# A state-space convolution with a gated low-rank layer behind it: tables formed as they lie from group 3 on, products of zeros at the start, and two short chains on GpSimd

## The chip, the cores and the metric

The kernel runs on one core of one Trainium2 chip. A core has a matrix engine (TensorE, PE in the profile, with its weight loads as PEld), a vector engine (VectorE, DVE), a scalar engine for activations and copies (ScalarE, ACT), a general engine (GpSimd, POOL) and a queue engine that issues transfers (SyncE, SP). They run side by side and wait for each other by semaphores. The metric is the device time of one execution in microseconds; lower is better. Before the change it is 955.25 us, the median of three runs from 955.22 to 955.43.

## The reference

```python
x = x + ffn(cond(x, length, log_dt, C, log_A_real, A_imag, D), A, B, Wr)

# cond: a state-space convolution, H = 64 heads, N = 64 states a head, 64 rows, L = 1024
A = -exp(log_A_real) + 1j * A_imag
dtA = A * exp(log_dt)[:, None]
Cs = Cc * (exp(dtA) - 1.0) / A
K = 2.0 * einsum('hn,hnl->hl', Cs, exp(dtA[:, :, None] * arange(L))).real
y = (causal convolution of x * mask with K) + x * mask * D
y = y * mask

# ffn: 64 experts of rank 16, 16 of them chosen for each token
scores = y @ Wr.T
gates = softmax(top_k(scores, 16)), 0 elsewhere
out = einsum('nkr,kdr->nd', einsum('nd,krd->nkr', y, A) * gates, B) * 2.0
```

All of it is computed in float32.

## The kernel before

**Tiling.** The 64 heads are worked on in eight groups of eight (`NG = 8`, `HG = 8`), and a group's heads in four pairs (`GP = 4`): the 64 states of two heads fill 128 partitions. The 1024 places of a row are cut into eight blocks of 128 (`P = 128`, `NBLK = 8`).

**The convolution of a group, `conv(g)` (L660).** Inside a block it is a product with a Toeplitz matrix `toep` (L695). Across blocks it goes over states. `into_states` (L631) multiplies the input of a pair by the table `bt`, which holds, for each of the 128 places of a block, the factor with which that place enters each state: two matmuls for each of the real and the imaginary part (L642, tile `pu`), and a copy by ScalarE into `s` (L647). `recur` (L674) carries the states from block to block on VectorE, by `turn`. `across` (L700) multiplies the states by the table `w` into the same PSUM banks `pc` as the Toeplitz product (L704), and VectorE multiplies the sum by the mask into `y` (L712). Group 0 does all this by itself; from group 1 on `begin(g)` (L650) forms the states of the next group at the end of the `conv` before.

**The tables, `tables(g)` (L241).** A generator, which is run step by step (to its next `yield`) from within `conv` of the group before. Its first eight steps make, for 129 places `lv` along the free axis and the states on the partitions, the magnitude `mag` (exponentials on ScalarE, L253), the angle `f` in turns (L255 and on, VectorE), its sines (L268 to L271, ScalarE) and from these the real and imaginary part of `w`. Then `w` is multiplied by each state's `alpha` and `nbeta`: two ScalarE products (L353) and two VectorE operations (helper line L400) a pair, into tiles `b` with the states on the partitions. Since the matmul into the states needs the places on the partitions, `turned_table` (L333) transposes them on TensorE, eight 128x128 transposes a group (L338, tile `pb`), and ScalarE copies them into `bt` (L340). After that come `turn`, the sum of `bt` over the states (`kernels_by_vector`, L304), which gives the convolution's kernel, and its way through DRAM into `toep` (L315 to L320).

The tiles `mag`, `f`, `k` and `sn` of `tables` exist once each (`tabp`, one buffer): a new tile of the same name waits until the old one has been read for the last time.

**The steps.** From group 1 on `conv(g)` runs `step(4)` after the recurrence of pairs 0 and 1 (L746), `step(6)` after that of pairs 2 and 3 (L755), and `step(1)` (L761) ahead of `begin(g + 1)`.

**The layer behind.** `first(g)` (L842) multiplies `y` by the first low-rank factor with seven products of half-size blocks in place of eight (`seven`, L577, the matmul of L587, tile `h`), `gates` (L766) makes the scores and the gates, GpSimd multiplies by the gates `gx` (L857), and `second` (L936) does the same with the second factor (L1095) for all groups at the end. The products of `first` are generators too and are laid between the steps of the next group's `conv`.

**The start.** VectorE and ScalarE follow an order written by hand here (`manual_schedule`, L438 and L440): `exp_parts` (L415) for the step sizes and decay rates, then, taken in turns by `together` (L403), the first steps of `tables(0)`, `real_part` (L472) and `angle` (L479), then `products` (L517), which ends with `alpha`, `nbeta` and `nalpha`. In the meantime TensorE adds quarters of the first factor by products with the identity (`factors_by_identity`, L187, L195), as the quarters land; ScalarE copies these sums (L200, L204).

**Order.** Where no order is written by hand, a scheduler sets each engine's order before the run, out of the program's order and estimated times. At run time each engine and each queue takes its instructions strictly in that order; SP's queue carries the loads of `x` (L147) and the transfers of `krows` and `toep`.

Of the kernel before, what the change touches and what calls it, by code (L numbers as in the profile page):

```python
# [37 lines left out]
F32 = mybir.dt.float32  # L38
I32 = mybir.dt.int32
AF = mybir.ActivationFunctionType  # L40
ALU = mybir.AluOpType
# [3 lines left out]
P = 128  # L45
NB = 64
NH = 64
L = 1024
# [14 lines left out]
NP = NH // 2  # L63
GP = HG // 2
NW = P + 1
NCH = NBLK - 1
# [3 lines left out]
MAGIC = 12582912.0  # L70
INV_HI = 5.0 / 32.0
INV_LO = INV2PI - INV_HI
HALF_IN = 0.49999997
# [19 lines left out]
def body(ctx: ExitStack, tc, x, xo, lens, par, dvec, dgrp, at, bm, wt, cst, out):  # L93
    nc = tc.nc
    V = nc.vector
    G = nc.gpsimd
# [90 lines left out]
    def factors_by_identity(a21, a22, a11, a12, out):  # L187


        s1, s2, s4 = (factor(wp, "wa", t) for t in ("s1", "s2", "s4"))  # L190
        out.extend((a11, a12, s4, a22, s1, s2, a21))
        banks = [ps_f.tile([P, L // 2], F32, tag="pf", name=f"sum_{k}") for k in range(KH)]

        def add(bank, a, first=False, last=False):
            nc.tensor.matmul(bank, lhsT=ident, rhs=a, start=first, stop=last, skip_group_check=True)  # L195

        for k in range(KH):
            add(banks[k], a21[:, k, :], first=True)
            add(banks[k], a22[:, k, :])
            nc.scalar.copy(s1[:, k, :], banks[k])  # L200
            yield
        for k in range(KH):
            add(banks[k], a11[:, k, :], last=True)
            nc.scalar.copy(s2[:, k, :], banks[k])  # L204
            yield
# [30 lines left out]

    tabs = {}
    turned = {}
    scales = {}

    def tables(g):  # L241
# [80 lines left out]
        def rows(ks, i, n):  # L322
# [5 lines left out]
            nc.sync.dma_start(toep[:, 2 * i : 2 * n, :],  # L328
                              bass.AP(row.tensor, row.offset, [[1, P], [KROW, 2 * (n - i)], [1, P]]))

        bbs, halves = [], []

        def turned_table(i, n):  # L333

# [4 lines left out]
                                        bbs[(i + m) // 2][:, (i + m) % 2, c, :], ident)  # L339
            nc.scalar.copy(bt[:, i : i + n, :], pb)  # L340

        for i in range(GP):
            j = j0 + i
            re, im = w[:, 0, i, :P], w[:, 1, i, :P]
            if i % 2 == 0:
                bb = tabp.tile([P, 2, 2, P], F32, tag=("sn", "k")[i // 2], name=f"b_{g}_{i}")
                bbs.append(bb)
            b = bb[:, i % 2]
            for c, by in enumerate((alpha, nbeta)):
                if g == 0:  # L350
                    ts(b[:, c, :], re, by[:, j : j + 1], ALU.mult)
                else:
                    nc.scalar.activation(b[:, c, :], re, AF.Copy, scale=by[:, j : j + 1])  # L353
            stt(b[:, 0, :], im, nbeta[:, j : j + 1], ALU.mult, b[:, 0, :], ALU.add)
            stt(b[:, 1, :], im, nalpha[:, j : j + 1], ALU.mult, b[:, 1, :], ALU.add)
            if g:
                if i % 2:
                    yield
                continue
            turned_table(i, 1)  # L360
            if i % 2:
                halves.append(kernels(bbs[i // 2 :], i - 1))
            if i == 3:
                rows(*halves[0])
            yield
        if g:
            turn, toep = others()
            for i in (0, 2):
                turned_table(i, 2)
            turned[g] = bt  # L370
            yield
# [12 lines left out]
    def new(name, w=NP, dtype=F32, keep=False):  # L384
        pool = const if keep else prep
        return pool.tile([P, w], dtype, tag=f"p_{name}", name=f"p_{name}")

    def tt(o, a, b, o_):
        V.tensor_tensor(out=o, in0=a, in1=b, op=o_)  # L389
        return o  # L390

    def ts(o, a, s1, o1, s2=None, o2=None):
        if o2 is None:
            V.tensor_scalar(out=o, in0=a, scalar1=s1, scalar2=None, op0=o1)
        else:
            V.tensor_scalar(out=o, in0=a, scalar1=s1, scalar2=s2, op0=o1, op1=o2)
        return o

    def stt(o, a, s, o1, b, o2):
        V.scalar_tensor_tensor(out=o, in0=a, scalar=s, in1=b, op0=o1, op1=o2)  # L400
        return o
# [10 lines left out]
        for _ in range(n):  # L412
            yield next(it, None)

    def exp_parts(xin, name, w, out):  # L415

        xc = ts(new(name + "x", w), xin, -87.0, ALU.max, 88.0, ALU.min)
        k = ts(new(name + "k", w), xc, LOG2E, ALU.mult)
        yield
        ts(k, k, MAGIC, ALU.add, MAGIC, ALU.subtract)  # L420
        yield
        stt(xc, k, -LN2_HI, ALU.mult, xc, ALU.add)
        yield
        stt(xc, k, -LN2_LO, ALU.mult, xc, ALU.add)
        s = new(name + "s", w, I32)
        ts(s, k, 127.0, ALU.add, 8388608.0, ALU.mult)
        yield
        q = ts(new(name + "q", w), xc, 1.0 / math.factorial(8), ALU.mult)
        for i in range(7, 0, -1):
            yield  # L430
            stt(q, q, 1.0 / math.factorial(i), ALU.add, xc, ALU.mult)
        out += [s.bitcast(F32), q]
# [5 lines left out]
    first_order.enter_context(tc.manual_schedule(engines={V.engine}))  # L438
    first_copies = ExitStack()
    first_copies.enter_context(tc.manual_schedule(engines={nc.scalar.engine}))  # L440
    log_both = par_sb[:, 0:2, :].rearrange("p a h -> p (a h)")
    a_im, c_re, c_im = (par_sb[:, i, :] for i in (2, 3, 4))
    parts = []
# [28 lines left out]
    def real_part():  # L472
# [3 lines left out]
        yield  # L476
        stt(em1, parts[0], -1.0, ALU.add, em1, ALU.add)

    def angle():  # L479
        ts(r, turns, MAGIC, ALU.add, MAGIC, ALU.subtract)  # L480
        yield
        tt(r, tu_hi, r, ALU.subtract)
        yield
        tt(r, r, tu_lo, ALU.add)
        yield
        ts(r, r, HALF_IN, ALU.min, -HALF_IN, ALU.max)
        nc.scalar.activation(sin, r, AF.Sin, scale=2.0 * math.pi)
        nc.scalar.activation(s2, r, AF.Sin, scale=math.pi)
        yield
        tt(den, a_re, a_re, ALU.mult)  # L490
        yield
        tt(t1, a_im, a_im, ALU.mult)
        yield
        tt(den, den, t1, ALU.add)
        yield
        V.reciprocal(rden, den)
        yield
        tt(s2, s2, s2, ALU.mult)
        yield
        ts(s2, s2, 2.0, ALU.mult)  # L500

    wa, wb = [], []
    marks = {}
# [13 lines left out]
    def products():  # L517
        ts(e_re, s2, -1.0, ALU.mult, 1.0, ALU.add)
        stt(e_im, em1, 1.0, ALU.add, sin, ALU.mult)
        yield  # L520
        tt(e_re, e_re, em1, ALU.mult)
        tt(t1, e_im, a_im, ALU.mult)
        tt(n_im, e_im, a_re, ALU.mult)
        yield
        tt(e_re, e_re, s2, ALU.subtract)
        yield
        tt(n_re, e_re, a_re, ALU.mult)
        tt(t2, e_re, a_im, ALU.mult)
        yield
        tt(n_re, n_re, t1, ALU.add)  # L530
        tt(n_im, n_im, t2, ALU.subtract)
        yield
        tt(n_re, n_re, rden, ALU.mult)
        tt(n_im, n_im, rden, ALU.mult)
        yield
        tt(alpha, c_re, n_re, ALU.mult)
        tt(t1, c_im, n_im, ALU.mult)
        tt(beta, c_re, n_im, ALU.mult)
        tt(t2, c_im, n_re, ALU.mult)
        yield  # L540
        tt(alpha, alpha, t1, ALU.subtract)
        tt(beta, beta, t2, ALU.add)
        yield
        ts(alpha, alpha, 2.0, ALU.mult)
        ts(nbeta, beta, -2.0, ALU.mult)
        ts(nalpha, alpha, -1.0, ALU.mult)

    together(products(), some(steps0, 2))
# [111 lines left out]
    def conv(g, steps, out):  # L660
# [39 lines left out]
        def across(i, s, pcs, pinned=False):  # L700
            for c in range(2):
                for hh in range(2):
                    o = hh * NS
                    m = nc.tensor.matmul(  # L704
                        pcs[hh][:, NB:], lhsT=w[o : o + NS, c, i, 1:],
                        rhs=s[o : o + NS, c].rearrange("p k b -> p (k b)"),
                        start=False, stop=(c == 1),
                    )
                    if pinned:
                        tc.keep_in_program_order(m)  # L710
            for hh in range(2):
                marks["y"] = V.tensor_tensor(  # L712
                    out=y[:, :, i // 2, 2 * (i % 2) + hh, :],
                    in0=pcs[hh].rearrange("p (k b) -> p k b", b=NB), in1=mask, op=ALU.mult)

        def step(n):
            for _ in range(n):
                next(steps, None)
# [14 lines left out]
        if g == 0:  # L733
            into_states(0, 2, bt, states, more)
            into_states(0, 3, bt, states, more)
            first_two = inside(0), inside(1)
            across(*first_two[0], True)
            across(*first_two[1])
            recur(2, 3)
            last_two = inside(2), inside(3)  # L740
            yield
            across(*last_two[0], True)
            across(*last_two[1])
            return
        yield
        step(4)  # L746
        yield 2

        first_two = inside(0), inside(1)
# [481 lines left out]
    def flat(t, i, w):  # L1231
        return t[:, i : i + w * HT].rearrange("p (k t) -> p k t", t=HT)
# [13 lines left out]
    n = 0  # L1246
# [84 lines left out]
```

## Time and profile before

One execution was taken by the profiler. Times are in us.

| | |
|---|---|
| median of three runs | 955.25 |
| the profiled execution: its time, and its span from first to last instruction | 955.27, 953.5 |
| TensorE busy (matmuls) | 942.5, 99% |
| VectorE busy | 714.3, 75% |
| GpSimd busy | 332.5, 35% |
| ScalarE busy | 150.8, 16% |
| transfers | 143.97 MB, mean 151 GB/s |
| transposes into `pb` (L338) | 64 instructions, 9.6 busy |
| copies into `bt` (L340), 128x512 | 14, 7.5 busy |
| ScalarE products into `b` (L353) | 56, 21.7 busy |
| VectorE operations into `b` (L400) | 64, 22.0 busy |
| recurrence (L400 into `s` and `s_more`) | 576, 172.7 busy |

Busy time is the union of an engine's instructions. A single instruction's time includes the pipeline's ends, so the distance between two starts is often shorter than the duration. A wait is named as "engine line waited for: us in total, times, longest". Helper lines stand for many operations: L389 is any VectorE operation with two tensors, L396 and L394 one with a tensor and numbers, L400 one with a tensor, a number and a tensor. The numbers of the tiles' copies are left out, so `was` is any tile of the first factor whose name begins so.

### The profile page before, as it was taken

To read this page: it belongs to the slowest core of one execution; us is meant where nothing else is said; L and a number is where in the kernel's file an instruction comes from. 1 tells how busy PE (TensorE), PEld (TensorE's weight loads), DVE (VectorE), ACT (ScalarE), POOL (GpSimd) and SP (SyncE) were. 2 spreads that over 40 slices of the span, in tenths; PEclk is the share of its full clock that TensorE was granted. 3 is DMA by queue.
4 is the path that set the end of the run, shared out by engine and by line. 5 is a ranking of instruction groups with operands and counts; after the bars stand their busy time and mean duration, and the time that the engine had idled before them with its cause. 6 is when DMAs were issued, how large, how long until landed. Compare 5 with 4: busy or idle time off the path is not lost. (4 is left out here: it accounts for less than half of the span.)

```text
span 953.5 us, 11891 instructions
## 1 busy us (share of the span) xinstructions
PE 942.5 (99%) x4259; PEld 725.4 (76%) x4259; DVE 714.3 (75%) x1697; ACT 150.8 (16%) x302; POOL 332.5 (35%) x285
## 2 busy tenths in 40 slices
PE   7999999999999999999999999999999999999998
PEld 2476767587587587587587688888888888888887
DVE  8899798695794795695594399869856865786674
ACT  5343233401401401311200000000000000000000
POOL 0212204042042041042132132257745554764565
PEclk9999999999999999999999999999999999999999
DMA  8815326235243244334323274653683475268332
GB/s 287 228 41 166 120 78 172 83 108 164 89 142 129 89 116 138 106 105 133 121 69 126 95 268 149 244 221 102 221 296 89 166 265 188 84 214 299 110 119 102
DMA packets 68985, 143.97 MB, mean 151 GB/s; under 512 B 9472, under 2 KB 20288, under 8 KB 68928
## 3 DMA queue, kind: packets, MB, share of 16 engines
q1 hardware_dynamic: 49420, 94.40, 29.5%
q0 software_dynamic: 16864, 47.22, 15.4%
q10 hardware_dynamic: 2644, 1.61, 0.6%
q8 instruction: 33, 0.54, 0.2%
q14 instruction: 24, 0.20, 0.1%
HBM read 94.89 MB, written 47.25 MB: 149 GB/s over the span
## 5 line engine op out<-in xcount | busy, mean ns | idle before, releaser
L400 DVE SCALAR_TENSOR_TENSOR s<-s,turn 128x64 f32<-128x64 f32 (+1 forms) x432 | 118.9, 320 | 3.5 <-ACT s L647 2.4
L857 POOL TENSOR_TENSOR hg<-h_p,gx 128x512 f32<-128x512 f32 x16 | 29.3, 1829 | 258.0 <-DVE h_p L400 251.9
L587 PE MATMUL h<-y,waa 128*128 128x256 f32 x512 | 118.7, 381 | 0.0
L587 PE MATMUL h<-y,was 128*128 128x256 f32 x512 | 116.5, 380 | 0.0
L587 PE MATMUL h<-ty,was 128*128 128x256 f32 x512 | 116.0, 379 | 0.0
L587 PEld LDWEIGHTS h<-y,waa 128*128 128x128 f32 x512 | 95.6, 190 | 20.0 <-issue 6.9
L587 PEld LDWEIGHTS h<-y,was 128*128 128x128 f32 x512 | 96.7, 190 | 15.0 <-issue 1.5
L587 PEld LDWEIGHTS h<-ty,was 128*128 128x128 f32 x512 | 97.1, 190 | 13.9 <-issue 0.8
L712 DVE TENSOR_TENSOR y<-pc,mask 128x512 f32<-128x512 f32 x64 | 41.1, 684 | 52.3 <-PE pc L704 52.3
L857 POOL TENSOR_TENSOR hg<-h_u,gx 128x512 f32<-128x512 f32 x32 | 46.7, 1460 | 78.8 <-DVE h_u L389 73.7
L1109 ACT COPY p<-s 128x512 f32<-128x512 f32 x28 | 16.4, 586 | 312.4 <-PE s L1095 312.4
L954 POOL TENSOR_TENSOR o<-o,acc_a 128x512 f32<-128x512 f32 x32 | 47.6, 1506 | 41.4 <-ACT acc_a L972 21.6
L389 DVE TENSOR_TENSOR h_u<-h,h_u 128x512 f32<-128x512 f32 x48 | 32.8, 683 | 35.3 <-PE h L587 35.3
L587 PE MATMUL h<-ty,waa 128*128 128x256 f32 x256 | 58.4, 381 | 0.0
L695 PE MATMUL pc<-x,toep 128*128 128x512 f32 x128 | 57.7, 594 | 0.0
L587 PEld LDWEIGHTS h<-ty,waa 128*128 128x128 f32 x256 | 48.2, 190 | 9.6 <-DVE y L712 3.3
L954 POOL TENSOR_TENSOR o<-o,b_room 128x512 f32<-128x512 f32 x32 | 49.1, 1556 | 9.8 <-DVE b_room L389 9.8
L830 POOL DMA_DIRECT2D gx<-gt_dram x56 | 33.9, 620 | 51.5 <-DMA gt_dram<-gt 51.5
L389 DVE TENSOR_TENSOR o<-o,s 128x512 f32<-128x512 f32 x50 | 34.1, 681 | 23.1 <-PE s L1095 17.9
L642 PE MATMUL pu<-x,bt 128*64 128x448 f32 x256 | 51.1, 545 | 0.0
L389 DVE TENSOR_TENSOR hg<-hg 128x512 f32<-128x512 f32 x64 | 42.5, 684 | 10.5 <-POOL hg L857 9.9
L954 POOL TENSOR_TENSOR o<-o,u 128x512 f32<-128x512 f32 x36 | 45.3, 1281 | 10.0 <-DVE u L389 9.7
(238 smaller groups left out, 1612.5 us busy)
## 6 DMA issues: line engine op xcount, KB each, us to landing
x<-in_x SPq DMA_DIRECT2D x32, 512.0 KB
hg_dram<-hg POOLq DMA_DIRECT2D x16, 1024.0 KB, 5.6
o<-in_xo SPq DMA_DIRECT2D x64, 256.0 KB
out<-o SPq DMA_DIRECT2D x63, 256.0 KB
gx<-gt_dram POOLq DMA_DIRECT2D x56, 256.0 KB, 4.8
qy<-hg_dram SPq DMA_DIRECT2D x28, 512.0 KB
r<-hg_dram SPq DMA_DIRECT2D x26, 512.0 KB
hg_dram<-hg POOLq DMA_DIRECT2D x16, 768.0 KB, 4.0
```

Of the source, the lines that this page charges most:

```text
L389: V.tensor_tensor(out=o, in0=a, in1=b, op=o_)
L400: V.scalar_tensor_tensor(out=o, in0=a, scalar=s, in1=b, op0=o1, op1=o2)
L587: nc.tensor.matmul(bank[:, ii, :], lhsT=fac[n - 1][:, k, (j + ii) * P : (j + ii + 1) * P], rhs=rf[n - 1][:, k, :], start=(first and ii == ...
L642: nc.tensor.matmul(pu[hh * NS : (hh + 1) * NS, :], lhsT=bt[:, i, (1 - c) * P + hh * NS : (1 - c) * P + (hh + 1) * NS], rhs=xt[:, hh, : NCH ...
L695: nc.tensor.matmul(pc, lhsT=toep[:, 2 * i + hh, :], rhs=xt[:, hh, :], start=True, stop=False)
L712: marks["y"] = V.tensor_tensor(out=y[:, :, i // 2, 2 * (i % 2) + hh, :], in0=pcs[hh].rearrange("p (k b) -> p k b", b=NB), in1=mask, op=ALU ...
L830: i = queue.dma_start(gx[:, ii, :], gt_dram[g, c * n : (c + 1) * n, :].unsqueeze(1).to_broadcast([n, RANK, TOK]),)
L857: G.tensor_tensor(out=o, in0=a, in1=b, op=op)
L954: tc.keep_in_program_order(G.tensor_tensor(out=o, in0=a, in1=b, op=op_))
L1109: nc.scalar.copy(p1, c11)
```

## The change

**Tables as they lie.** From group 3 on (`DIRECT = 3`) `bt` isn't made by transposing. At the end of group 0 `parameter_rows` transposes five small tables of parameters (128 partitions x 32) on TensorE, so that each becomes rows, and writes them to DRAM (`rows_of`). For groups 3 to 7 `tables_as_they_lie` reads, for each of the five, the 512 values of the group into all 128 partitions, 256 KB, in SP's queue, and computes magnitude, angle, sines and the products with `alpha` (`by` there begins as row 3) and `nbeta` (row 4) on [128 places, 4 x 128 states] straight into `bt`. It uses the buffers of `mag`, `f`, `sn` and `k` again. The loop that multiplied `w` by `alpha` and `nbeta`, and `turned_table`, are not run for these groups. The table of `w` itself is still made as before. `conv(g)` runs eight steps instead of four behind its first recurrence when the next group is one of these.

**Products of zeros.** A tile `idle` is set to zero on VectorE at the very start; TensorE multiplies it by itself twice ahead of the first sum and twice behind it, into banks that are not read.

**Chains on GpSimd.** Four operations of `angle` on 128x32, and the three that make `den`, go from VectorE to GpSimd. The factor 2 of `alpha` and `nbeta` is put into `rden`, the one of `s2` into its square, and the sign of `nbeta` into `beta`.

```diff
@@ factors_by_identity
+        def unread(n):
+            for i in range(n):
+                bank = ps_c.tile([P, L // 2], F32, tag="pc", name="unread")
+                tc.keep_in_program_order(
+                    nc.tensor.matmul(bank, lhsT=idle[:, :P], rhs=idle, start=True, stop=True))
+        unread(2)
...
         for k in range(KH):
-            add(banks[k], a21[:, k, :], first=True)
+            i = add(banks[k], a21[:, k, :], first=True)
+            if k == 0:
+                tc.keep_in_program_order(i)
+                unread(2)
@@ parameters
+    DIRECT = 3
+    rows_of = dram.tile([5, NP, P], F32, tag="rows_of", name="rows_of")
+    def parameter_rows(room):
+        values = (dt_re, tu_hi, tu_lo, scales["alpha"], scales["nbeta"])
+        r = room[:NP].rearrange("p c k b -> p (c k b)")[:, : 5 * P].rearrange("p (k q) -> p k q", q=P)
+        for i, n in ((0, 3), (3, 2)):
+            pr = ps_k.tile([NP, n, P], F32, tag="pk", name=f"par_rows_{i}")
+            for m in range(n):
+                nc.tensor.transpose(pr[:, m, :], values[i + m], ident)
+            nc.scalar.copy(r[:, i : i + n, :], pr)
+        nc.scalar.dma_start(rows_of.rearrange("k j q -> j k q"), r)
@@ tables
+        def tables_as_they_lie():
+            def flat(t):
+                return new(t, f"r{t}").rearrange("p i l -> p (i l)")[:, : GP * P]
+            def row(t, n):
+                nc.sync.dma_start(
+                    t, rows_of[n, j0 : j0 + GP, :].rearrange("j q -> (j q)").partition_broadcast(P))
+            mag, f, lo, k = (flat(t) for t in ("mag", "f", "sn", "k"))
+            place = feat[:, 0:1]
+            row(f, 1)
+            row(mag, 0)
+            row(lo, 2)
+            yield
+            nc.scalar.activation(mag, mag, AF.Exp, scale=place)
+            ts(f, f, place, ALU.mult)
+            ts(k, f, MAGIC, ALU.add, MAGIC, ALU.subtract)
+            yield
+            tt(f, f, k, ALU.subtract)
+            stt(f, lo, place, ALU.mult, f, ALU.add)
+            ts(f, f, HALF_IN, ALU.min, -HALF_IN, ALU.max)
+            nc.scalar.activation(k, f, AF.Sin, scale=math.pi)
+            nc.scalar.activation(lo, f, AF.Sin, scale=2.0 * math.pi)
+            nc.scalar.activation(k, k, AF.Square)
+            nc.scalar.activation(k, k, AF.Copy, scale=-2.0, bias=1.0)
+            by = flat("f")
+            row(by, 3)
+            yield
+            tt(lo, mag, lo, ALU.mult)
+            tt(k, mag, k, ALU.mult)
+            nby = flat("mag")
+            row(nby, 4)
+            yield
...
+            tt(b0, re, by, ALU.mult)
+            tt(b1, im, by, ALU.mult)
+            yield
+            tt(re, re, nby, ALU.mult)
+            tt(im, im, nby, ALU.mult)
+            tt(b0, b0, im, ALU.add)
+            tt(b1, re, b1, ALU.subtract)
+            yield
+        if g >= DIRECT:
+            yield from tables_as_they_lie()
-        for i in range(GP):
+        for i in range(GP if g < DIRECT else 0):
...
-            for i in (0, 2):
+            for i in (0, 2) if g < DIRECT else ():
                 turned_table(i, 2)
@@ start
+    idle = prep.tile([P, L // 2], F32, tag="idle", name="idle")
+    V.memset(idle, 0.0)
@@ angle
-        ts(r, turns, MAGIC, ALU.add, MAGIC, ALU.subtract)
-        yield
-        tt(r, tu_hi, r, ALU.subtract)
-        yield
-        tt(r, r, tu_lo, ALU.add)
-        yield
-        ts(r, r, HALF_IN, ALU.min, -HALF_IN, ALU.max)
+        G.tensor_scalar(out=r, in0=turns, scalar1=MAGIC, scalar2=MAGIC, op0=ALU.add, op1=ALU.subtract)
+        G.tensor_tensor(out=r, in0=tu_hi, in1=r, op=ALU.subtract)
+        G.tensor_tensor(out=r, in0=r, in1=tu_lo, op=ALU.add)
+        G.tensor_scalar(out=r, in0=r, scalar1=HALF_IN, scalar2=-HALF_IN, op0=ALU.min, op1=ALU.max)
...
-        tt(den, a_re, a_re, ALU.mult)
-        yield
-        tt(t1, a_im, a_im, ALU.mult)
-        yield
-        tt(den, den, t1, ALU.add)
-        yield
+        G.tensor_tensor(out=den, in0=a_re, in1=a_re, op=ALU.mult)
+        G.tensor_tensor(out=den2, in0=a_im, in1=a_im, op=ALU.mult)
+        G.tensor_tensor(out=den, in0=den, in1=den2, op=ALU.add)
         V.reciprocal(rden, den)
         yield
-        tt(s2, s2, s2, ALU.mult)
-        yield
-        ts(s2, s2, 2.0, ALU.mult)
+        ts(rden, rden, 2.0, ALU.mult)
+        yield
+        stt(s2, s2, 2.0, ALU.mult, s2, ALU.mult)
@@ products
-        tt(beta, c_re, n_im, ALU.mult)
+        stt(beta, c_re, -1.0, ALU.mult, n_im, ALU.mult)
...
-        tt(beta, beta, t2, ALU.add)
-        yield
-        ts(alpha, alpha, 2.0, ALU.mult)
-        ts(nbeta, beta, -2.0, ALU.mult)
+        tt(nbeta, beta, t2, ALU.subtract)
+        yield
         ts(nalpha, alpha, -1.0, ALU.mult)
@@ conv
             across(*last_two[1])
+            parameter_rows(fourth[0].tile([P, 2, NCH, NB], F32, tag="s_more", name="par_rows"))
             return
         yield
-        step(4)
+        step(4 if g + 1 < DIRECT else 8)
```

## The prediction

> **What bounds the kernel now.** I read the page first (busy shares, slices), then TensorE's own waits, then the timeline of one group in the steady stage, engine by engine, then the first 30 us. The columns of the first lines are busy us, share of the span and instructions; below them, tenths in 40 slices.
>
> ```profile
> PE 942.5 (99%) x4259; PEld 725.4 (76%) x4259; DVE 714.3 (75%) x1697; ACT 150.8 (16%) x302; POOL 332.5 (35%) x285
> ...
> PE   7999999999999999999999999999999999999998
> ...
> DVE  8899798695794795695594399869856865786674
> ```
>
> TensorE (PE) is short of work in the first slice only. Its list of waits says the same: 7.6 us in all, of which the first three lines make 6.5, all before 21 us.
>
> ```profile
> PE sum L195 <- DMA was<-in_at: 4.2, 1, 4.2
> PE sum L195 <- DMA waa<-in_at: 1.2, 1, 1.2
> PE pb L338 <- DVE b L400: 1.1, 2, 0.8
> PE s L1095 <- DVE acc_a L389: 0.5, 1, 0.5
> ```
>
> So after some 30 us time is the sum of TensorE's work, and what is taken from that work is won, as long as nothing makes it wait. Before that it waits for VectorE (DVE). The steady stage, TensorE's timeline (start, us, engine, line, operation, tiles, count), at the seam between two groups:
>
> ```profile
> 245.24 1.67 PE L704 MATMUL pc<-s_more,w 64*128 64x448 f32 x8
> 246.84 1.09 PE L338 MATMUL pb<-cst_sb,b 128*128 128x128 f32 x8
> 247.77 0.59 PE L587 MATMUL h<-y,waa 128*128 128x256 f32 x2
> ```
>
> The eight transposes hold TensorE from 246.84 to 247.77, 0.93 us; the 1.09 has the pipeline's end in it. The same block starts again at 320.24, so a group lasts 73.4 us. VectorE's slack in that period, from the table of stretches (length, then busy us of PE, PEld, DVE, ACT, POOL):
>
> ```profile
> 247.00:294.00 47.00, 47.00 (x224) 35.40 (x224) 45.67 (x146) 15.18 (x32) 12.15 (x14) 1.00 0.31 100
> 294.00:321.00 27.00, 27.00 (x117) 18.04 (x116) 9.27 (x15) 0.65 (x2) 5.22 (x5) 1.00 0.43 147
> ```
>
> **Part 1, the tables of groups 3 to 7.** *Removed, per group*: eight transposes (0.93 us of TensorE); two copies of them by ScalarE (ACT L340, 1.07 us for both); eight ScalarE products (L353, 0.39 each, 0.29 apart); eight VectorE L400 on 128x128, 0.264 apart, 2.1 us. TensorE: 5 x 0.93 = **-4.65 us**. I take all of it. A lower bound of the gain is 0, if the matmuls into the states (pu, L642), which now come first, have to wait for their banks. They should not: pair 0 takes the banks that the products of 245.43 to 246.72 (VectorE, L712) free, and pair 1 starts 1.6 us later, at 248.4, when the second two (246.94 to 248.23) are done.
>
> *Added, per group, on VectorE*: three tensor-scalar operations on 128x512 (nearest row: 0.42 long, 0.34 apart on 128x516) and ten with two tensors (0.68 long, 0.60 apart): 1.0 + 6.0 = 7.0 us, net +4.9 us. Cover: VectorE is busy 9.27 of the 27 us before the next seam, 17.7 us idle. Without that cover it would be 5 x 4.9 = 24.5 us on the path. *On ScalarE*: five activations (0.63 each) and at most two table loads (1.28 each), 5.7 us, against 3.4 removed; it is busy 16%. Cost taken: 0.
>
> *DMAs*: five rows spread over 128 partitions, 256 KB each, in SP's queue, for each of five groups. The nearest row is gx<-gt_dram, also 256 KB spread over partitions: 4.8 us from issue to landing. In SP's queue they pass the x loads, and the x loads pass them:
>
> ```profile
> 294.77 2.09 SPq L147 DMA_DIRECT2D x<-in_x  x2
> 315.42 2.08 SPq L147 DMA_DIRECT2D x<-in_x  x2
> ```
>
> The first three rows can start when this group's mag, f and sn are read for the last time, the products w at 286.09 to 287.4 in the trace of before, and in the changed order (eight steps instead of four ahead of the second recurrence) earlier, at 262 or so. From 287.4 on, the late case: landing 292.2; exponential and the first operations 2 us; sines 3 us; the fourth and fifth row 4.8 us more, 302; six products 3.6 us: the table lies ready at about 306, 14 us before 320.24. While VectorE waits for a row, what is queued behind it are h_u and h_p (which free TensorE's banks of products) and y. A wait of 2 us is covered by the four banks (3.45 us of products each); I take 0, and price a longer one as a rival.
>
> **Part 2, rows of the parameters.** Five transposes at the end of group 0, at the 0.116 us of a transpose (0.93/8): +0.58 us, between 0 (TensorE is idle 0.59 us between 20 and 30 us in the table of stretches) and 0.58. I take **+0.58**. Two copies and a DMA on ScalarE lie in its 10 us of waiting before 44 us; the room they borrow (s_more) is filled again only at the matmuls of 73 to 80 us.
>
> **Part 3, products of zeros.** Four products of 128x512. Two consecutive ones start at 9.28 and 10.98, 1.70 us each; later they run at 0.86 (twelve instructions, two per product, in 5.51). The memset is before VectorE's first wait (3.29). Two of them fill TensorE's 4.20 us of waiting for data, two the 1.17 before 7.41. Even if all ran at 1.70 from 1.5 us on, the real second product would start at 10.0 rather than 7.41; eleven left at 0.86 end by 19.5, still before the 19.87 at which VectorE lets the next matmul start. Value: 0 either way, because this stage ends on VectorE, not on the sums. If that cover were gone they would cost up to 2.6 us.
> The Trainium skill ("TensorE: Matmul & The Clock Gate", Part 1) says full rate comes after about 3.4 us of activity and is lost after an idle window as long, which would explain those 1.70 and 0.86. It also speaks against the change: sums done sooner leave TensorE idle for longer ahead of 19.87. By the rule half rate there would cost at most an estimated 1.7 us; by the rows I count nothing.
>
> **Part 4, GpSimd chains.** VectorE in the first 20 us (its timeline):
>
> ```profile
> 10.44 0.18 DVE L394 TENSOR_SCALAR p_fk<-p_fx 128x32 f32<-128x32 f32 x1
> 10.53 0.17 DVE L396 TENSOR_SCALAR p_r<-p_turns 128x32 f32<-128x32 f32 x1
> 10.62 0.69 DVE L389 TENSOR_TENSOR f<-f,k 128x516 f32<-128x516 f32 x1
> ...
> 19.86 0.40 PEld L338 LDWEIGHTS pb<-cst_sb,b 128*128 128x128 f32 x2 [1.58 <-DVE b L400]
> ```
>
> The angle's operations fill slots of 0.10 us between others. Four leave before the clamp of f (12.94), but the reciprocal (0.26), a doubling and the square of s2 (0.09 each) come forward in their place: +0.08. Behind it the seven-fold chain is spaced 0.22 by dependence, so the others that leave there were free and only the reciprocal's stall goes: together -0.05. Two scalings at the end (18.78, 18.89) go: -0.21. Sum **-0.25 us**. Bounds: -2.0 (nine fewer, each at the dependent 0.22), and upwards GpSimd's lateness: seven operations on 128x32, which no row shows. GpSimd's rows are 0.175 for 1x1 and 1.27 for 128x512; in proportion 0.24. The third waits for tu_lo (9.24); with five from there the denominator is ready at 10.5, and VectorE asks for it at 11.2. At 1.27 each it is ready at 15.6, 4.4 us late. I take 0, since 32 columns are nearest to the 1x1 row.
> The skill ("GPSIMD Engine Reference", 2.1 Instruction dispatch) warns that the first call to freshly loaded code pays about 6 us with no instruction shown. The first two-tensor operation of GpSimd in this trace (76.22) took 1.27 like the next, behind an idle 3.25, so no more than 3.25 can hide there. With the page's figure the sum would be about 4 us worse.
>
> **Sum.** -4.65 + 0.58 - 0.25 = -4.3 us. The profiled execution took 955.27 (span 953.5 and 1.77 around it), 0.02 above the median of 955.25: **950.9 us**. Its own range: from 949.2 (parameter transposes in gaps, start 1.2 better) to 952.9 (half a GpSimd delay).
>
> **Rivals.** *A, GpSimd late*: VectorE stands at the reciprocal. For it: first calls, unknown sizes. Against: 0.24 in proportion. At 1.27 each, 950.9 + 4.4 = 955.3; at half of that 953.1. Chance 0.16, two thirds of it within 0.2% of before, a third faster.
> *B, slower: rows late in SP's queue.* If the fifth row is queued behind the second two x loads, it goes out at 317.5, lands at 322.3, and four products of 0.60 end at 324.7, 4.5 us after the seam; TensorE stands at pu for that long in five groups: +22.3, 973.2 us. It decides from 0.86 us per group (4.3/5) on. For it: one in-order queue, two more round trips, and VectorE fuller by 4.9 us. Against: 14 us of slack. Chance 0.14.
> *C, nothing won*: pu waits for its banks as long as the transposes took, 955.2. Against it stand the times of L712 above. This is the case that the change does not do what it says; it shares A's 0.16.
>
> **Numbers.** Forecast 0.70, A with C 0.16, B 0.14. A measurement here tells 0.2% (1.9 us) from no change. Faster: 0.70 + 0.05 = 0.75; within: 0.11; slower: 0.14. The range takes the forecast's own and most of A, 949.2 to 956.0; B is left out.
>
> **What would show it.** Right: no pb but group 0 to 2's; busy TensorE down by about 4; pu directly behind pc at each seam; VectorE's idle before the seam down to some 13 us; first pb at about 19.6. Wrong: a wait of PE or PEld pu for DVE bt (B), of DVE rden for POOL den (A), of pu for y (C).

## The result and the profile after

The changed kernel takes 962.08 us (median of five runs, 961.89 to 964.32) against 955.25: a ratio of 1.0078, 95% interval 1.0067 to 1.009. The change makes the kernel 0.8% slower. The profiled execution took 961.97, with a span of 960.0 against 953.5. TensorE is busy for 1.2 us more than before (943.7 against 942.5), where the prediction looked for some 4 less.

First the page of the changed kernel (busy us, share, count; below, tenths in 40 slices of 24 us).

```profile
PE 943.7 (98%) x4232; PEld 725.2 (76%) x4232; DVE 736.6 (77%) x1714; ACT 162.4 (17%) x289; POOL 335.3 (35%) x292
...
PE   8999999799999999999999999999999999999998
...
PEclk9999999899999999999999999999999999999999
```

A new slice below 9 stands in PE's row, the eighth (168 to 192 us), and in the same slice the granted clock is down. TensorE's list of waits names it, and the timeline gives its place:

```profile
PE h L674 <- ACT h_p L689: 5.3, 1, 5.3
PE pu L729 <- DVE y L799: 1.5, 1, 1.5
...
PE psc L870 <- ACT sh L866: 1.2, 2, 0.8
```

```profile
163.56 3.62 PE L674 MATMUL h<-ty,was 128*128 128x256 f32 x16
172.48 6.02 PE L674 MATMUL h<-y,waa 128*128 128x256 f32 x16 [5.30 <-ACT h_p L689]
...
186.67 6.23 PE L729 MATMUL pu<-x,bt 128*64 128x448 f32 x32 [1.53 <-DVE y L799]
```

TensorE stands 5.30 us, the block behind takes 6.02 where its neighbour takes 3.62, and it stands another 1.53 at the seam of group 3. The table of stretches shows the clock of that block (length; PE, PEld, DVE, ACT, POOL busy; granted clock, DMA share, GB/s):

```profile
160.00:170.00 10.00, 7.18 (x34) 5.97 (x32) 6.14 (x11) 3.53 (x5) 0.00 (x0) 1.00 0.61 196
170.00:180.00 10.00, 7.52 (x20) 5.56 (x21) 9.27 (x18) 4.28 (x9) 2.09 (x2) 0.66 0.10 39
```

Everywhere else the change does what it says. The seam that the prediction showed, one group's end at some 250 us, has no pb any more, and pu follows pc:

```profile
254.40 1.67 PE L791 MATMUL pc<-s_more,w 64*128 64x448 f32 x8
256.00 6.23 PE L729 MATMUL pu<-x,bt 128*64 128x448 f32 x32
```

So one place, 25 us long, eats the gain of five seams; the matmuls of the scores, psc, wait another 1.2 us at two seams. What happens there is read backwards. ScalarE's copy h_p, for which TensorE waits, stands in ScalarE's queue behind the magnitudes of group 4. These wait for the buffer of mag, which holds row 4 until VectorE's product of 169.96 has read it, and this product is late because its rows are. 14 us earlier ScalarE had already waited for the magnitude row of group 3 (SP's and ScalarE's timelines):

```profile
146.24 0.32 SPq L363 DMA_DIRECT2D rmag<-rows_of  x1
156.61 1.28 ACT L372 ACT_TABLE_LOAD   x1 [11.61 <-DMA rmag<-rows_of]
...
170.68 1.28 ACT L279 ACTIVATE mag<-cst_sb,p_dtre 128x129 f32<-128x129 f32 x4 [1.94 <-DVE rsn L466]
171.87 0.56 ACT L689 COPY h_p<-h 128x512 f32<-128x512 f32 x1
```

VectorE of the changed kernel in the same stretch, and under it what answers to it before the change:

```profile
161.12 0.69 DVE L466 TENSOR_TENSOR rsn<-rmag,rsn 128x512 f32<-128x512 f32 x1 [5.41 <-ACT rsn L380]
...
166.34 0.69 DVE L466 TENSOR_TENSOR bt<-rsn,rf 128x512 f32<-128x512 f32 x1 [2.73 <-DMA rf<-rows_of]
...
171.77 0.68 DVE L466 TENSOR_TENSOR h_u<-h,h_u 128x512 f32<-128x512 f32 x1
...
182.73 0.69 DVE L952 TENSOR_TENSOR hg<-h,gx 128x512 f32<-128x512 f32 x1 [3.42 <-PE pc L782]
185.53 0.48 DVE L471 TENSOR_SCALAR rf<-rf,cst_sb 128x512 f32<-128x512 f32 x1 [2.11 <-DMA rf<-rows_of]
185.93 2.48 DVE L799 TENSOR_TENSOR y<-pc,mask 128x512 f32<-128x512 f32 x4
```

```profile
159.99 0.69 DVE L389 TENSOR_TENSOR h_u<-h,h_u 128x512 f32<-128x512 f32 x1 [0.34 <-PE h L587]
...
170.35 0.69 DVE L864 TENSOR_TENSOR hg<-h,gx 128x512 f32<-128x512 f32 x1 [2.69 <-PE h L587]
...
175.48 1.29 DVE L712 TENSOR_TENSOR y<-pc,mask 128x512 f32<-128x512 f32 x2 [4.44 <-PE pc L704]
```

In the changed kernel the store of the sums hg (GpSimd's timeline) comes between the late h_u and the late hg:

```profile
177.66 0.83 POOL L948 DMA_DIRECT2D hg_dram<-hg  x1 [3.86 <-DVE hg L466]
```

h_u is 11.8 us later than before, the first operation into the next hg 12.4, the y 10.4. I took the ScalarE copy for the cause at first (theory Q: one place in ScalarE's queue); the experiments led from there to VectorE.

### The profile page after: what moved, and what is told of

It reads as the page before. It is cut to its first block, busy times and chain, and to the rows that moved or that the text cites. A ratio compares the mean times of both kernels' runs of the same rounds, so it can differ in the third digit from the quotient of the medians.

```text
span 960.0 us, 11911 instructions
## 1 busy us (share of the span) xinstructions
PE 943.7 (98%) x4232; PEld 725.2 (76%) x4232; DVE 736.6 (77%) x1714; ACT 162.4 (17%) x289; POOL 335.3 (35%) x292
## 5 line engine op out<-in xcount | busy, mean ns | idle before, releaser
L477 DVE SCALAR_TENSOR_TENSOR s<-s,turn 128x64 f32<-128x64 f32 (+1 forms) x432 | 109.8, 304 | 1.6 <-ACT s L734 1.4
L945 POOL TENSOR_TENSOR hg<-h_p,gx 128x512 f32<-128x512 f32 x16 | 32.1, 2005 | 189.2 <-DVE h_p L477 177.6
L945 POOL TENSOR_TENSOR hg<-h_u,gx 128x512 f32<-128x512 f32 x32 | 44.4, 1389 | 76.6 <-DVE h_u L466 73.3
L477 DVE SCALAR_TENSOR_TENSOR s_more<-s_more,turn 128x128 f32<-128x128 f32 x144 | 51.5, 358 | 0.0
```

The lines of the kernel that those rows point to most:

```text
L945: G.tensor_tensor(out=o, in0=a, in1=b, op=op)
```

## The experiments

Each ran four to eleven times beside the kernel before, whose median was 955.12 in the first batch of four, 955.23 in the next two and 955.20 in the last. Diffs are against the changed kernel unless said otherwise. `tc.issue_after(i)` puts what is issued in its block behind instruction i on i's engine.

**e4 and e16, the start and the parameters' rows alone.** e4: `DIRECT = 8` and no call of `parameter_rows`; e16: `DIRECT = 8` only.

> Only the start of the change: products of zeros and the chains on GpSimd; all tables by transposes as before, no rows of parameters. By the prediction -0.25 us, 955.0; by the trace of the changed kernel, in which the first pu starts at 21.71 instead of 21.84, -0.1: 955.1. Rival (the start costs something, GpSimd or the zeros): 955.5 to 956.5.

> The changed start, the products of zeros and the transposes of the parameters into rows, but no group uses the rows: all tables are transposed as before. Forecast's term: 955.4 (e4) + 0.58 = 956.0. Rival (the transposes fall into gaps of TensorE): 955.4. The loss of the changed kernel must not show here in either case: under 957.

955.41 (ratio 1.0002, 0.9993 to 1.0011) and 955.83 (1.0006, 0.9997 to 1.0015). Chains, zeros and parameters cost 0.6 us between them (955.83 against 955.20), which the interval doesn't tell from nothing; the loss is in the tables.

**e1, ScalarE's copy ahead of group 4's magnitudes.**

```diff
-        nc.scalar.copy(p1, c11)
+        i = nc.scalar.copy(p1, c11)
+        if name == "h1" and j == 2:
+            marks["p"] = i
...
+        with ExitStack() as behind:
+            if g == DIRECT + 1:
+                behind.enter_context(tc.issue_after(marks["p"].ins))
             for i in range(GP):
                 nc.scalar.activation(mag[:, i, :], lv, AF.Exp, scale=dt_re[:, j0 + i : j0 + i + 1])
```

> One ScalarE instruction changes place: the copy h_p (of the product of group 1, second half) stands ahead of the four exponentials of group 4's table instead of behind them; nothing else moves. Theory Q (queue): in the changed kernel TensorE's wait of 5.3 us and the slow block behind it (6.0 instead of 3.6 us) come from that copy standing behind exponentials that wait for the buffer mag, which holds row 4 until 169.96. Then both go: 962.1 - 5.3 - 2.4 = 954.4 us. Theory V (VectorE too full): VectorE is late with all that TensorE needs there, the wait on ScalarE is only the last of several; then TensorE waits for something else at the same place and the time stays at 960 or above.

963.25 (1.0087, 1.0073 to 1.01). The 5.3 us wait is gone, and the other has grown by more (its list of waits):

```profile
PE pu L734 <- DVE y L804: 8.5, 1, 8.5
```

Theory Q falls: the ScalarE wait hid a longer one at the same seam.

**e2, five unread products of 128x512 in the 5.3 us gap**, placed ahead of `product(2, c11)` for that one half.

> Five products that nobody reads (128x512, 0.86 us each, 4.3 us) are put into the idle 5.3 us of TensorE in the changed kernel; the copy stays where it is, so the wait is as long. Theory C (clock): the block of 16 matmuls behind the gap took 6.0 us instead of 3.6 because TensorE had stood still; kept busy it takes 3.6 again and the time falls by 2.4 us to 959.7, although work was added. Rival: the block is slow for another reason (operands late, banks late): 962.1 or more.

964.25 (1.0094, 1.008 to 1.0108). Its TensorE timeline:

```profile
167.11 4.46 PE L702 MATMUL filler<-mask,cst_sb 128*128 128x512 f32 x10
171.40 3.64 PE L674 MATMUL h<-y,waa 128*128 128x256 f32 x16
...
186.13 9.19 PE L733 MATMUL pu<-x,bt 128*64 128x448 f32 x32 [4.46 <-DVE y L803]
```

The block takes 3.64 instead of 6.02: its slowness was the clock after the idle time. The kernel wins nothing, as the seam still ends on y, and now pu runs slow behind a wait of 4.46.

**e3, rows 3 and 4 loaded early into the two halves of bt**, so that no row waits for a buffer of an earlier step; the same six products, in place.

```diff
+            into(b0, 3)
+            into(b1, 4)
             row(f, 1)
...
-            by = flat("f")
-            row(by, 3)
...
-            nby = flat("mag")
-            row(nby, 4)
...
+            re, im, both = (lay(t) for t in (k, lo, f))
+            tt(both, im, b0, ALU.mult)
+            tt(b0, re, b0, ALU.mult)
             yield
+            tt(re, re, b1, ALU.mult)
+            tt(b1, im, b1, ALU.mult)
+            tt(b0, b0, b1, ALU.add)
+            tt(b1, re, both, ALU.subtract)
```

> Rows 3 and 4 (alpha and nbeta) are read straight into the two halves of bt, which is free by then, together with the first three rows; the buffers mag and f are not needed for them, and the same six products run in place. Theory Q: mag is free some 7 us earlier, the exponentials and the copy behind them don't wait, and VectorE's wait of 2.7 us for row 3 goes too: 954.4, or 953 if pu's wait of 1.5 us for y goes with it. Theory V: the operations of VectorE are as many as before, 960 or above.

960.25 (1.0051, 1.0039 to 1.0064). The ScalarE wait goes, pu waits 7.4 us for y. In the changed kernel, e1 and e3 VectorE's first operation on group 4's angle row stands directly ahead of the y, waiting 2.1 to 2.2 us for its row (theory W); in e2 it waits 6.25 us, with one hg between it and the y.

**e5, e6, e7, this operation behind the y**: on the changed kernel, on e3, on e1.

```diff
+            with ExitStack() as behind:
+                if g == DIRECT + 1:
+                    behind.enter_context(tc.issue_after(last_y[DIRECT - 1].ins))
-            ts(f, f, place, ALU.mult)
+                ts(f, f, place, ALU.mult)
...
+        last_y[g] = marks["y"]
```

> Only the order of VectorE's queue around one instruction is changed: the first operation on the angle row of group 4 stands behind the last multiplication by the mask (y) of group 2 instead of ahead of it. Theory W: this row operation waits for a row that cannot be fetched before the sines of group 4's own table w have read the buffer, and the four y queued behind it free the banks that the matmuls into the states need; so the wait of pu for y (1.5 us after the change, up to 8.5 in the two kernels with the earlier waits removed) goes. In this kernel the 5.3 us wait for the ScalarE copy and the 2.4 us of half rate behind it remain: 962.1 - 1.5 = about 960.5. Rival R (rows late, wherever they are used): the row operation waits as long behind y, and the recurrence of group 3, now behind the row operation, is late instead: no change, 962 or more.

> Rows 3 and 4 go early into the two halves of bt as in e3, and the y of group 2 stand ahead of the first row operation of group 4 as in e5. Theory W: both waits go and nothing takes their place: e3's 960.25 less its wait of 7.4 and the 2.1 by which the block of pu behind it was stretched, about 950.8 (range 950 to 953), faster than before by about 0.4%. Rival R: the wait moves a third time, to the recurrence of group 3 or the scores: 957 or more.

> Two swaps in queues and nothing else: ScalarE's copy of the product of group 1 ahead of group 4's magnitudes as in e1, and the y of group 2 ahead of the first row operation of group 4 as in e5. All of the changed kernel's transfers, buffers and operations remain. Theory W: 963.25 - 8.5 - 2 = about 952.8 (951 to 955). If so, the whole loss is the places of two instructions in in-order queues. Rival R (transfers and buffers are late, not places): 958 or more.

e5 960.44 (1.0056, 1.0043 to 1.0068), as W said; e6 956.84 (1.0017, 1.0008 to 1.0026) and e7 961.29 (1.0068, 1.0056 to 1.0081), 6.0 and 8.5 us above it. W is one link only: without the 5.3 us at ScalarE, pu still waits 4.4 and 7.4 us for the y, now behind `hg<-h,gx` (the profiled run of e6 is its slowest, 958.76). In e6 this operation starts at 180.41, GpSimd having issued the store of the previous hg at 175.34; in e7 at 183.49 after 178.40; in the changed kernel at 182.73 after 177.66. Always 5.1 us: the pool of hg has one buffer, and VectorE waits for its store to land. (Before the change it is 5.25 us, 170.35 after 165.10, but there the trace puts the wait down to TensorE's product, which ended at 170.31.) The store comes after the four sums hg, these after GpSimd's product, this after h_u, and h_u stands in VectorE's queue behind the products of group 3's rows (theory V).

**e8, tables as they lie from group 4 on** (`DIRECT = 4`).

> Tables formed as they lie from group 4 on instead of group 3: group 3 keeps its transposes. Theory S (the loss belongs to group 3 alone, because its rows fall into the short period of 58 us of group 2's convolution with the spreading of gates beside it): 955.25 - 4 x 0.93 + 0.58 = about 952.1. Rival F (the loss belongs to whichever group comes first, since two successive groups chain on one buffer): the same waits one group later, 958 to 963.

960.41 (1.0054, 1.004 to 1.0068; the profiled run is the fastest, 958.6): rival F, the loss goes to the next first group. Theory S falls: this group's table is made in a period of 69.96 us before the change (176.88 to 246.84), not of 59.4. VectorE there:

```profile
245.12 0.49 DVE L471 TENSOR_SCALAR rf<-rf,cst_sb 128x512 f32<-128x512 f32 x1 [4.29 <-DMA rf<-rows_of]
245.52 0.68 DVE L466 TENSOR_TENSOR h_u<-h,h_u 128x512 f32<-128x512 f32 x1
```

The wait is 4.29 us with h_u behind it, and pu waits for y for 4.3. The row isn't slow here, it lands within 3.7 us: it goes out only at 241.44, when ScalarE's sine (240.80, 0.62 long) has read its buffer.

**e9, e10, e11, the first product of group 3's rows behind h_u**: on the changed kernel, on e6, on e7. **e12**: `DIRECT = 4` with e3's loads and both orders in every group.

```diff
+            with ExitStack() as behind:
+                if g == DIRECT:
+                    behind.enter_context(tc.issue_after(u2_done[g - 2, 0].ins))
-            tt(lo, mag, lo, ALU.mult)
+                tt(lo, mag, lo, ALU.mult)
             tt(k, mag, k, ALU.mult)
...
-            tt(u2, c12, u2, ALU.add)
+            u2_done[g, j] = V.tensor_tensor(out=u2, in0=c12, in1=u2, op=ALU.add)
```

> Only the order in VectorE's queue: the first product of group 3's rows (magnitude by sine) stands behind the sum h_u of group 1's first low-rank products instead of ahead of it, and the y of the first two pairs and the sums hg with it. Theory V (one chain of single buffers): the row products wait for ScalarE's exponential and sines, which wait for late rows (5.4 us), and for row 3 (2.7 us); h_u behind them is 12 us late (171.8 against 160.0 before), so GpSimd's product, the four sums hg, the store to DRAM (issued at 177.7 against 165.1) and with its landing 4.9 us later the only buffer of hg; VectorE stands for it (182.7) with the y behind it. Then here h_u is at about 160 to 163, the store at 166 to 168, and VectorE's wait for the buffer at 182.7 goes. ScalarE's copy is not moved, so 5.3 + 2.4 us remain: about 960.5. Rival W (only the row operation of group 4 ahead of y): hg still waits until 182, 962.

> e6 (rows 3 and 4 straight into bt, y ahead of group 4's first row operation) with the order of e9 added. Theory V: no wait of pu for y (4.4 us in e6) and no slow block behind it (2.7): 956.84 - 4.4 - 2.7 = about 949.8, between 949 and 952.5. Rival N (the rows' landing holds the group's work in any order: the next thing that uses them is late, the recurrence, the table bt, or the sums): 955 or more.

> All transfers, buffers and operations of the changed kernel, three swaps of queue places: ScalarE's copy (e1), y (e5), h_u (e9). Theory V: e7 without its wait of 7.4 us and the 1.3 by which the block behind it was slower: 961.29 - 8.7 = about 952.6, between 950 and 954.5. If so the whole loss is three places in in-order queues and no transfer needs to be faster. Rival N: 957 or more.

> Tables as they lie from group 4 on, rows 3 and 4 straight into bt, and in every group the row operations behind h_u and y. Theory V: in e8 group 5's first row operation stood 4.3 us for its row with h_u, hg and y behind it; with that gone 960.41 - 4.3 - 1.7 = 954.4 at most, and 955.25 - 4 x 0.93 + 0.58 = 952.1 if no wait is left. Rival N: 957 or more.

e9 963.45 (1.0084, 1.0071 to 1.0098) and e11 960.45 (1.0055, 1.0041 to 1.0069): missed. e10 954.23 (0.9987, 0.9978 to 0.9996): the first below the kernel before, though 4.4 above what was expected. e12 956.7 (1.0016, 1.0007 to 1.0025): short as well; pu waits 0.6 at three seams there, psc 2.0 in all, and not all of its rest is accounted for. Why e9 missed is in its VectorE timeline:

```profile
162.10 0.69 DVE L469 TENSOR_TENSOR rk<-rmag,rk 128x512 f32<-128x512 f32 x1 [4.66 <-ACT rk L382]
165.60 0.69 DVE L469 TENSOR_TENSOR bt<-rk,rf 128x512 f32<-128x512 f32 x1 [2.81 <-DMA rf<-rows_of]
...
167.41 0.68 DVE L967 TENSOR_TENSOR h_u<-h,h_u 128x512 f32<-128x512 f32 x1
...
181.10 0.69 DVE L956 TENSOR_TENSOR hg<-h,gx 128x512 f32<-128x512 f32 x1 [1.24 <-DMA hg_dram<-hg]
```

The edit held back one product; the scheduler put the other, rk, into its place, and a bt behind it. The waits stayed ahead of h_u. Here the trace names the store as what `hg<-h,gx` waits for.

**e13, e14, e15, all products of group 3's rows behind the four sums**: on e7 (all transfers and buffers as in the changed kernel), on e6, and e14 with ScalarE's exponential of the later groups' rows behind its copy of the scores. `sum_factors()` issues the four sums; `marks["sum"]` is the last of them.

```diff
+            with ExitStack() as behind:
+                if g == DIRECT:
+                    sum_factors()
+                    behind.enter_context(tc.issue_after(marks["sum"].ins))
-            tt(lo, mag, lo, ALU.mult)
-            tt(k, mag, k, ALU.mult)
+                tt(lo, mag, lo, ALU.mult)
+                tt(k, mag, k, ALU.mult)
...
+            with ExitStack() as behind:
+                if g > DIRECT:
+                    behind.enter_context(tc.issue_after(marks["sh"].ins))
-            nc.scalar.activation(mag, mag, AF.Exp, scale=place)
+                nc.scalar.activation(mag, mag, AF.Exp, scale=place)
```

> All transfers, buffers and operations of the changed kernel; only queue places are changed: e1's and e5's swaps, and all products of group 3's rows behind the four sums hg of group 1's first half and the y of its two pairs. Theory V: h_u at about 160 as before the change, the store of hg out at about 165.5, its buffer free at 170.5, VectorE's first operation into it without a wait behind the rows' products, y right behind pc, no wait of pu: 961.3 (e7) - 7.4 - 1.4 = about 952.5, between 950.5 and 954.5. Rival N (rows as such: row 4, which follows the products into the buffer they free, then lands so late that the table bt, group 4's magnitudes or its angle are late): 957 or more.

> e10 with all products of group 3's rows behind the four sums hg. Theory V: e10's last wait of pu (1.7 us) goes: 954.2 - 1.7 = about 952.5, faster than before by 0.3%. Rival N: 954 or more.

> e14, and ScalarE's exponential of the rows of groups 4 to 7 stands behind its copies of states and scores instead of among them. The waits of psc for ScalarE's copy (2.2 us in e10, three times) were behind this exponential, which waits for its row (2.9 us at 183.6 in e10). Theory V: they go, 952.5 - 2.2 = about 950.3, the time that was forecast for the change. Rival N: the row's table comes later by as much and VectorE waits: 952.5 or more.

e13 955.98 (1.0009, 1.0 to 1.0018): 6.1 us of the changed kernel's 6.9 of loss go by queue places alone, with all of its transfers and operations, so VectorE isn't simply too full. The chain of V is gone: h_u is back at its old time, and `hg<-h,gx` doesn't wait. It is 3.5 above the value expected, as rival N has its part: row 4 goes only into the buffer of mag when the products have read it (issued 166.41), and VectorE stands for it with hg and y behind (pu waits 1.7 and 1.0 at two seams, psc 1.7 in all). Its VectorE timeline:

```profile
160.35 0.69 DVE L476 TENSOR_TENSOR h_u<-h,h_u 128x512 f32<-128x512 f32 x1 [2.23 <-PE h L684]
...
172.07 0.69 DVE L476 TENSOR_TENSOR rk<-rk,rmag 128x512 f32<-128x512 f32 x1 [2.50 <-DMA rmag<-rows_of]
...
175.42 0.68 DVE L966 TENSOR_TENSOR hg<-h,gx 128x512 f32<-128x512 f32 x1
```

e14, without that row in mag, takes 951.73 (0.9964, 0.9951 to 0.9978), and e15 949.96 (0.9944, 0.9931 to 0.9956): faster than both kernels. The first line of e15's list of waits, and its seam of group 3:

```profile
PE unread L198 <- DVE idle L545: 1.5, 1, 1.5
```

```profile
175.66 1.67 PE L804 MATMUL pc<-s_more,w 64*128 64x448 f32 x8
177.26 6.23 PE L742 MATMUL pu<-x,bt 128*64 128x448 f32 x32
```

What is left stands in the first 26 us, but for 0.31 us at 536 and 0.53 at 628, two waits that the kernel before has too; psc no longer waits.

## Why the prediction was wrong, point by point

**The transposes (-4.65): right in mechanism, undersized.** In e15, where nothing waits, the steady distance between two groups' psh is 72.17 us (324.21 to 396.38) against 73.40 before (327.98 to 401.38): 1.23 a group, not 0.93. Of the other 0.30, 0.22 lie in the 32 products of pu, which took 6.45 and take 6.23. The transposes aren't what slowed them: the pu of 118.96, behind transposes too, took 6.24 before the change. From the next seam on ScalarE put a sine of the next group's table among its copies out of pu (before the change, its timeline), and TensorE's last loads for pu waited 0.77 us for these copies; in e15 the eight copies follow each other without it.

```profile
182.71 0.64 ACT L268 ACTIVATE sh<-f 128x516 f32<-128x516 f32 x1
183.25 1.38 ACT L647 COPY s<-pu 128x448 f32<-128x448 f32 x3
```

The span of e15, 947.7, is 5.8 below before, where the sum said 4.3. By the medians it is 5.2, since the runs of e15 last 1.94 to 2.03 us longer than their spans, and not the 1.77 that the prediction added.

**The transfers and waits of Part 1 (taken as 0): this step failed**, in the sentence "A wait of 2 us is covered by the four banks". VectorE waited 5.41 and 2.73 us for rows ahead of h_u, and the seam lost 9.2 us by it and by ScalarE's copy (5.30, 2.40 and 1.53). The table itself was in time: in the steady group its last operation starts at 305.44, 23 us ahead of pu (329.14), and in group 3 at 171.16, 15 ahead (186.67). What came late was the other work in the queues. Three things in it:

- *The period.* The slack was worked out in a group of 73.4 us. Group 3's table is made in the one before: 59.4 us from pb to pb (117.50 to 176.88), with the x loads and eight spread gates in its middle. That is not needed for a loss: e8 has one of the same kind in a period of 69.96.
- *The landing.* I took 4.8 us from gx. In the steady groups that held: rmag issued at 331.77 is there by 335.96. In group 3 rmag, issued at 146.24, ended ScalarE's wait at 156.61, 10.4 us later; eight gx (2 MB) went out from 142.97 on and 1 MB of x at 151.72, and the transfer engines' busy share is 1.05 from 150 to 160. That these transfers slowed the row is likely, but no run here takes them away; in e8 the row that is waited for is late by its buffer instead.
- *What stands behind a wait.* I named h_u and y as queued behind a row operation and then priced only TensorE's banks. The wait is passed on almost in full (h_u 11.8 us late, y 10.4) through single buffers: h_u, GpSimd's product, the sums, the store, the only buffer of hg, then y, then the banks of pu. e13 shows this chain by taking it away. ScalarE has one of its own, priced at 0 as well: h_p behind the magnitudes, which wait for mag; e1 and e3 take it away.

From e15's span to that of the changed kernel it is 12.3 us: 5.30 at h_p, 2.40 of slow clock, 1.53 at pu, 1.16 at psc, together 10.4. Of the other 1.9, 0.9 come behind the start of TensorE's last block (953.98 and 942.56, 11.4 apart); the rest I can't name line by line.

**Rival B** had the right sign and mechanism (rows late, pu waits) but the wrong place: a fixed delay in each of five groups, by SP's queue, 22.3 us. Pu never waits for bt, and at groups 4 to 7 not at all. **Rival C** is refuted by the seam at 254.40. **Rival A** too: GpSimd's operations on 128x32 take 0.23 to 0.57 us, the denominator is ready at 9.1, and VectorE's reciprocal starts without a wait at 11.17. (Half of A's delay gives 953.1, as stated with A, and not the 952.9 that ends the forecast's own range.)

**Parameter transposes (+0.58)**: e16 less e4 is +0.42. **Start (-0.25)**: e4 gives +0.3 against its own before, within what can't be told from nothing; the first pu comes at 21.71 in the changed kernel, at 21.87 in e4, at 21.84 before, so no gain is shown. **Zeros (0)**: nothing speaks against it. The first sum starts later (5.03 for 4.20), but the first pb, at 19.49, still waits for VectorE. No run has the zeros without the chains.

## What to carry to other kernels

Before new work is laid into an engine's idle time, list what stands behind its waits in the in-order queue and follow each to its next single buffer: idle time covers busy time, but not a wait for a transfer. Work the slack out in the first and the tightest period that the new work touches, not only in the steady one, with the transfers that run there and the buffers that they wait for. Here the scheduler had placed the readers of late rows ahead of ready work; pin the whole reader behind that work, not its first instruction (e9 against e13).

## What the runs showed of the hardware

After an idle time of 4.3 us or more TensorE's next block ran slow: 6.02 for 3.62, pu 7.6 to 9.2 for 6.23, with a granted clock of 0.66 in the stretch; after 1.53 and 1.68 us (changed kernel, e13) pu took its full-rate 6.23. (e9's 28 products of 8.34 stand behind only 2.11 us, but the clock was still at 0.50 from the 5.01 us of idle time just before.) The Trainium skill ("TensorE: Matmul & The Clock Gate", Part 1) puts the idle window at about 3.4 us, which lies between these.

A wait's price is thus not its length: e2's 4.46 us at pu cost about 3 us more in the block behind it, and e7's 7.38 us only 1.35 more. In 1 us stretches the clock stands at 0.50 for some 6.0 us of e2's block, 4.7 of the changed kernel's and 2.7 of e7's, and about half of that is lost each time (2.96, 2.40, 1.35).

The skill ("GPSIMD Engine Reference", 2.1 Instruction dispatch) has the first call of freshly loaded code pay some 6 us. No run here shows it: GpSimd's first two-tensor operation on 128x32, at 3.16 in the changed kernel, took 0.24, behind an idle 2.23 that ended as its input landed (VectorE's first operation on the same input starts at 3.11).
